# Deformable convolution of one Trainium2 core: samples on 32x32 tiles, pixels by lanes, y offsets by transfers

## The chip, the cores and the metric

The kernel runs on one core of a Trainium2 chip. The metric is the device time of one execution in microseconds (us), lower is better. The kernel before took 5572.15 us (median of 3 runs, 5569.34 to 5579.46).

TensorE (PE in the profile, with its weight loads in a row of their own, PEld) multiplies, VectorE (DVE), ScalarE (ACT) and GpSimd (POOL) work element by element, and SyncE (SP) issues nearly all transfers. Each engine runs its own instructions in order and waits for the others by semaphores.

## The reference, cut to what matters

```python
x = x + _L0_conv_ref(_gn(x), w_off, b_off, w_def)    # layer 0: the change is here
x = x + _L1_conv_ref(_gn(x), W)                      # scan over rows with a 9-tap convolution
x = x + _L2_conv_ref(_gn(x), ...)                    # messages
x = x + _L3_conv_ref(_gn(x), ...)                    # gated triangle product

def _L0_conv_ref(x, w_off, b_off, w_def):            # x: [4, 128, 128, 128]
    offset = einsum('bchw,oc->bohw', x, w_off) + b_off      # 72 = 4 groups x 9 taps x {dy, dx}
    py = offset[dy] + ky - 1 + row ; px = offset[dx] + kx - 1 + column
    val = bilinear sample of x[group] at (py, px)    # 32 channels per group, zero outside
    return relu(einsum('bgckhw,ogck->bohw', val, w)) # 3x3 convolution over the samples
```

`_gn` is a group norm with 32 groups. A bilinear sample is a sum over pixels of tent(y distance) x tent(x distance) x pixel, with tent(d) = max(0, 1 - |d|); the kernel uses this form.

## The kernel before

The four layers run one after the other. The deformable layer (`deform_layer`, line 181) takes the first 3300 us of the span or so. The two layers after it, and a general path for far offsets that lies in a branch not taken, are not touched.

*Blocks.* `deform_layer` walks over 172 blocks, 4 images x 43 blocks of 3 rows (RY = 3). Within a block the 130 padded columns fall into pieces of 4 (RX = 4), 33 of them. An output of a piece can only see 5 x 6 = 30 pixels (SY x SX, NS), called lanes, in each of 4 groups: 120 lanes. So the samples of a piece are one matmul (`sample`, line 521): 120 lanes x 128 channels of pixels as weights, whose blocks off the diagonal of groups are zero, and 120 x 108 products of tents `m` (9 taps x 3 rows x 4 columns) as the moving operand, in f32. One block has 33 of them, in 8 steps `i` of four (the last of five), each step into one PSUM tile `v_ps`, of which there are two. `keep_samples` (ACT, line 531) copies a step's tile to `v`.

*Tents.* The offsets, split into three bf16 parts each with the maximum of each beside it, lie in DRAM (`offs`). `load_places` brings them for a block, shifted by tap, into four groups of 25 partitions of `places` (2 tap slots x {y, x}). `spread_offsets` (line 498) turns them into tents on the 120 lanes by small bf16 matmuls with 25 rows: per tap three for y (130 columns) and four for x (99 columns with a stride of 4), 63 for a block, into tiles `t_ps` of two banks, two of them. The taps come in five batches (`SLOTS`: four of two taps, one of one), at steps given by `DONE`. `tents` then copies the y part out of PSUM (ACT, line 508) and multiplies it with the x part into `m` (DVE, line 510), once for each of the 9 taps.

*Convolution.* `convolved` is a generator: 15 f32 matmuls over `v` of the block before and the present one (line 579), cut into pieces of 3, 2, 2, 2, 2, 2, 2 and an end (line 552, DVE: relu and residual). Each step takes one piece.

*Preparing.* `prepared` runs beside it, one step at a time (`step`), at least 2 rows and mostly up to 26 rows ahead: it transposes 4 rows of x (line 370), norms them (ACT, line 373), writes 8 rows as table `tab` in DRAM with each pixel at its lanes (lines 378 and 380, pieces of 512 B, from `rows`), and computes the offsets: the product (line 385), corrections on DVE and POOL (390, 393), the bf16 parts (409, 415, 418), their range (412, 414), and after 8 rows a transfer to `offs`. `load_pixels` (line 466) gathers a block's pixel tile from `tab` in pieces of 128 B (33 x 120), into one of two tiles.

*Order.* The order of instructions on every engine is the order in which the Python code issues them (`manual_schedule`, line 680). For each block n the loop issues: the pixel load of block n+1; then for i in 0..7: at i = 3 `load_row(n + 2)` (the `places`), the spread batch due for block n+1, `keep_samples` of the step before, one piece of the convolution, `sample`, the multiplies of the batch, group norm statistics (`count`), and one or two steps of `prepared`. The engines' own queues are in this order too; SP issues the loads and the stores in it.

Of the kernel before, what the change touches and what calls it, by code (L numbers as in the profile page):

```python
# [42 lines left out]
LANES = NS * NG  # L43
# [6 lines left out]
SLOTS = [(0, 6), (1, 7), (2, 8), (3, 5), (4,)]  # L50
# [130 lines left out]
def deform_layer(tc, c, small, x, w_off, b_off, w_def, x1, tabs, offs):  # L181
# [13 lines left out]
    NB = RY * PADW  # L195
    with ExitStack() as ctx:
        wp = ctx.enter_context(tc.tile_pool(name="l0w", bufs=1))
        ps_g = ctx.enter_context(tc.tile_pool(name="l0ps_g", bufs=1, space=PSUM))
        ps_t = ctx.enter_context(tc.tile_pool(name="l0ps_t", bufs=2, space=PSUM))
# [4 lines left out]
        NPH = NPY + NPX  # L204
        keep = ctx.enter_context(tc.tile_pool(name="l0keep", bufs=2))
# [9 lines left out]
        places = [wp.tile([P, len(SLOTS), RY, OW], BF16, name=f"places_{i}") for i in range(3)]  # L215
        last = wp.tile([P, 3, 1, OW], BF16, name="places_last")
        pixels = [wp.tile([P, NXB + 1, P], F32, name=f"pixels_{i}") for i in range(2)]
        parts = wp.tile([2 * NL, NPART, 2 * RO * OW], BF16, name="parts")

        def rims():  # L220

            zero = two.tile([P, 2 * SX * P], F32, name="zero", tag="m")
            nc.vector.memset(zero, 0.0)
            zrow = zero[0 : NXB + 1]
            zoff = zero[0 : 2 * NL, 0 : NPART * OW].bitcast(BF16)
            zoff = zoff.rearrange("p (n l) -> p n l", n=NPART)
            for b in range(B):
                t = tabs[b].rearrange("x (r s) c -> x r s c", s=SX)
                nc.scalar.dma_start(
                    t[:, 0:2].rearrange("x r s c -> x (r s c)"), zrow  # L230
                )
                nc.scalar.dma_start(
                    t[:, S + 2 : S + 3].rearrange("x r s c -> x (r s c)"), zrow[:, 0 : SX * P]
                )
                for xb, s0, s1 in ((0, 0, 2), (NXB, 2, SX)):
                    nc.scalar.dma_start(
                        t[xb : xb + 1, 2 : 2 + S, s0:s1].rearrange("x r s c -> (x r) (s c)"),
                        zero[0:S, 0 : (s1 - s0) * P],
                    )
                rows_ = offs[b].rearrange("(p n) l -> p n l", n=NPART)  # L240
                nc.scalar.dma_start(rows_[:, :, 0 : 2 * OW], zoff)
                nc.scalar.dma_start(rows_[:, :, (S + 2) * OW :], zoff)

        def tables():

            awayi = two.tile([NG, NPH, LANES], I32, name="awayi", tag="x1c")
            for i in range(NPY):
                nc.gpsimd.iota(
                    awayi[:, i], pattern=[[0, NG], [1, SY], [0, SX]], base=-1 - i,
                    channel_multiplier=0,  # L250
                )
            for i in range(NPX):
                nc.gpsimd.iota(
                    awayi[:, NPY + i], pattern=[[0, NG * SY], [1, SX]], base=-1 - i,
                    channel_multiplier=0,
                )
# [5 lines left out]
                fill=64.0, base=0, channel_multiplier=-NS,  # L262
# [3 lines left out]
                fill=64.0, base=NS - 1, channel_multiplier=NS,  # L266
            )
            picks = one.tile([NG, 3, 4, 32], F32, name="picks", tag="rows")
            for i, sign in enumerate((-1.0, 1.0, 1.0)):
                nc.gpsimd.memset(picks[:, i], sign)  # L270
# [17 lines left out]
            for t in (*pixels, parts):  # L288
                nc.gpsimd.memset(t, 0.0)
            yield  # L290
            picks16 = one.tile([NG, 3, P], BF16, name="picks16", tag="ve")
            nc.vector.tensor_copy(picks16, picks.rearrange("g k q r -> g k (q r)"))
            kinds = two.tile([NG, 3, NPH * LANES], BF16, name="kinds", tag="m")
# [10 lines left out]
            n = NPH * LANES // 3  # L304
            for h in range(3):
                if h % 2 == 0:
                    tp = ps_t.tile([P, 2, 512], F32, name="t_ps")
                at = slice(h * n, (h + 1) * n)
                for i in range(3):
                    nc.tensor.matmul(  # L310
                        tp[:, h % 2, 0:n], lhsT=picks16[:, i], rhs=kinds[:, i, at],
                        start=i == 0, stop=i == 2,
                    )
                nc.scalar.copy(to[:, at], tp[:, h % 2, 0:n])
# [43 lines left out]
        def prepared(b, y0):  # L358

            table = tabs[b].rearrange("x (r s) c -> x r s c", s=SX)  # L360
# [4 lines left out]
            for h in range(0, RC, RO):  # L365
                if h % (2 * RO) == 0:
                    rows = one.tile([P, 2 * RO, P], F32, name="rows")
# [5 lines left out]
                nc.scalar.activation(rows[:, h0 : h0 + RO], pt, AF.Identity, bias=t, scale=s)  # L373
                if h0:
                    r0 = 2 + y0 + h - RO
                    for q in range(RX):
                        src = rows[q:S:RX]
                        nc.sync.dma_start(table[0:NXB, r0 : r0 + 2 * RO, q + 2, :], src)
                        if q >= 2:
                            nc.sync.dma_start(  # L380
                                table[1 : NXB + 1, r0 : r0 + 2 * RO, q - 2, :], src
                            )
# [6 lines left out]
                off = one.tile([2 * NL, RO, S], F32, name="off")  # L389
# [8 lines left out]
                p0 = h % (2 * RO)  # L398
                at = slice(p0 * OW, (p0 + RO) * OW)

                def to(i):
                    return parts[:, i, at].rearrange("p (r c) -> p r c", c=OW)[:, :, 2 : S + 2]

                def high(t):
                    halves = t.rearrange("p r c -> p (r c)").bitcast(BF16)
                    return halves.rearrange("p (r c two) -> p r c two", r=RO, two=2)[:, :, :, 1]

                rest = one.tile([2 * NL, RO, S], F32, name="rest")
                nc.scalar.copy(to(0), high(off))
                nc.gpsimd.tensor_tensor(rest, off, high(off), ALU.subtract)  # L410
                flat = off.rearrange("p r c -> p (r c)")
                nc.vector.tensor_reduce(ranges[:, 0, n : n + 1], flat, AX.X, ALU.max)
                yield
                nc.vector.tensor_reduce(ranges[:, 1, n : n + 1], flat, AX.X, ALU.min)
                nc.scalar.copy(to(1), high(rest))
                nc.gpsimd.tensor_tensor(to(2), rest, high(rest), ALU.subtract)
                yield
                nc.vector.tensor_scalar(
                    parts[:, NSPLIT:, at], parts[:, 0:NSPLIT, at], 0.0, None, ALU.max
                )  # L420
                if p0:
                    r0 = y0 + h - p0 + 2
                    nc.sync.dma_start(
                        offs[b].rearrange("(p n) l -> p n l", n=NPART)[
                            :, :, r0 * OW : (r0 + 2 * RO) * OW
                        ],
                        parts,
                    )
                    ready[b] = y0 + h + RO
                    yield  # L430
                yield

        def shifted(b, d, k, n, row, count):

            ky, kx = divmod(k, 3)
            wide = (S + 4) * OW
            first = (d * NK + k) * NG * NPART
            whole = offs[b]
            return bass.AP(
                whole.tensor, whole.offset + first * wide + (row - ky + 2) * OW + 2 - kx,  # L440
                [[wide, NG * NPART], [NG * NPART * wide - 1, n], [1, count]],
            )

        def load_places(b, j):
            t = places[(b * NYB + j) % 3]
            for d in range(2):
                for q, slot, k, n in ((0, 0, 0, 3), (0, 3, 3, 2), (1, 0, 6, 3), (1, 3, 5, 1)):
                    p1 = 64 * d + 32 * q + 1
                    nc.sync.dma_start(
                        t[p1 : p1 + KROWS - 1, slot : slot + n].rearrange("p k r c -> p k (r c)"),  # L450
                        shifted(b, d, k, n, RY * j, RY * OW),
                    )
            if j + 1 == NYB:
                for d in range(2):
                    p1 = 64 * d + 33
                    nc.sync.dma_start(
                        last[p1 : p1 + KROWS - 1].rearrange("p k r c -> p k (r c)"),
                        shifted(b, d, 6, 3, PADW - 1, OW),
# [3 lines left out]
        def load_pixels(b, j):  # L462
            t = pixels[(b * NYB + j) % 2]
            for g in range(NG):
                nc.sync.dma_start(
                    t[g * NS : (g + 1) * NS, :, g * CG : (g + 1) * CG],
                    tabs[b][:, RY * SX * j : RY * SX * j + NS, g * CG : (g + 1) * CG].rearrange(
                        "x l c -> l x c"
                    ),
                )  # L470
# [3 lines left out]
        def spread_offsets(src, slot, taps, rows):  # L474

            tps, todo = [], []
            for q in taps:
                tp = ps_t.tile([P, 2, 512], F32, name="t_ps")
                tps.append(tp)
                for d in range(2):  # L480
                    p0 = 64 * d + 32 * q
                    wide = OW if d else PADW
                    to = tp[0:LANES, d, 0 : rows * wide].rearrange("p (r c) -> p r c", c=wide)
                    mov = src[p0 : p0 + KROWS, slot]
                    if d == 0:
# [1404 lines left out]
```

## Time and profile before

| | |
|---|---|
| median of 3 runs | 5572.15 us |
| profiled execution: its own time, its span | 5567.76 us, 5565.9 us |
| mean granted TensorE clock | 0.971 |
| deformable layer, in the span | up to about 3300 us |
| busy: PE, PEld | 93%, 80% |
| busy: DVE, ACT, POOL | 55%, 49%, 14% |
| 700 to 2900 us (120 blocks, counted by their outputs): one block | 18.33 us |

The profile is one execution, recorded by the hardware. A row such as "L521 PE MATMUL v_ps<-m,pixels 120\*128 120x108 f32 x11352 | 1462.3, 273 | 3.6" names the line of the kernel, the engine, the operation, output and inputs, the shapes, how many, then busy time in us and the mean of one in ns, and the idle time just before with what ended it. An f32 matmul leaves two pairs of records (a weight load and a matmul each), a bf16 matmul one. Matmuls overlap, so that a mean of 273 ns is how long one is in the pipeline, and not how far apart two of them start; for that, the start times of single records are compared.

### The profile page before, as it was taken

The page shows a single profiled execution, that of the slowest core. Times are in us where ns is not written, and L with a number is a line of the kernel's source. Part 1 is how long each engine was busy: PE and PEld are TensorE (multiplying, and loading weights), DVE is VectorE, ACT ScalarE, POOL GpSimd, SP SyncE. Part 2 cuts the span into 40 slices and gives each one's busy share as a digit, 9 for nine tenths or more (in the row PEclk, how much of TensorE's full clock was granted, in tenths as well). Part 3 has the DMA queues.
Part 4 walks back from the last instruction along what each step waited for, and adds up shares of the span by engine and source line. Part 5 has one row for each costly group of instructions (what it writes and reads, how often), then busy time and mean ns, then how long its engine had stood idle before and what let it go on. Part 6 is the DMA issues. An engine that isn't in the chain of part 4 may idle for free. (4 is left out here: it accounts for less than half of the span.)

```text
span 5565.9 us, 112097 instructions
## 1 busy us (share of the span) xinstructions
PE 5163.0 (93%) x42401; PEld 4438.1 (80%) x42401; DVE 3079.9 (55%) x10450; ACT 2721.1 (49%) x5802; POOL 787.0 (14%) x698
## 2 busy tenths in 40 slices
PE   2899999999999999999999989999989889898896
PEld 1778888888888888888888878999967768577686
DVE  6544444554444644444433337888876574764844
ACT  1345555445554455554544432333345475664755
POOL 2021111001111011111100002222210010110102
PEclk9899999999999999999999989999989999999999
DMA  4555555555555555554543423233232352642525
GB/s 142 146 129 137 128 136 122 127 118 135 133 131 119 131 112 137 129 141 113 124 78 76 76 56 91 91 107 103 91 100 92 97 195 80 207 147 82 203 95 169
DMA packets 1138394, 671.46 MB, mean 121 GB/s; under 512 B 737133, under 2 KB 1003566, under 8 KB 1121206
## 3 DMA queue, kind: packets, MB, share of 16 engines
q1 hardware_dynamic: 1127664, 657.77, 45.2%
q8 instruction: 338, 5.54, 0.4%
q10 hardware_dynamic: 10182, 6.43, 0.4%
q14 instruction: 210, 1.72, 0.1%
HBM read 382.88 MB, written 281.11 MB: 119 GB/s over the span
## 5 line engine op out<-in xcount | busy, mean ns | idle before, releaser
L510 DVE TENSOR_TENSOR m<-ty,t_ps 120x390 f32<-120x390 f32 x1548 | 805.0, 557 | 1497.2 <-ACT ty L508 1496.0
L521 PEld LDWEIGHTS v_ps<-m,pixels 120*128 120x128 f32 x11352 | 1436.1, 194 | 86.0 <-issue 8.7
L521 PE MATMUL v_ps<-m,pixels 120*128 120x108 f32 (+1 forms) x11352 | 1462.3, 273 | 3.6 <-ACT v L531 3.5
L531 ACT COPY v<-v_ps 128x432 f32<-128x432 f32 x1376 | 719.7, 523 | 1268.7 <-PE v_ps L521 1265.8
L579 PE MATMUL conv_ps<-v,wdef 128*128 128x128 f32 (+2 forms) x5160 | 1301.8, 378 | 6.5 <-DVE x1c L552 5.9
L579 PEld LDWEIGHTS conv_ps<-v,wdef 128*128 128x128 f32 x5160 | 812.8, 192 | 256.0 <-issue 21.7
L508 ACT COPY ty<-t_ps 120x390 f32<-120x390 f32 x1560 | 688.2, 489 | 176.9 <-PE t_ps L498 169.5
L498 PE MATMUL t_ps<-places,spread 25*120 25x99 bf16 (+1 forms) x10836 | 520.0, 259 | 62.1 <-DVE m L510 37.8
L498 PEld LDWEIGHTS <-spread 25*120 25x120 bf16 x10896 | 338.9, 136 | 224.5 <-issue 124.6
L1639 PEld LDWEIGHTS proj_ps<-wcat,X 128*128 128x128 f32 x4096 | 473.2, 192 | 19.1 <-issue 18.9
L393 POOL TENSOR_TENSOR off<-off,koff 72x512 f32<-72x512 f32 x128 | 162.1, 1266 | 2294.1 <-DVE off L390 2215.8
L1639 PE MATMUL proj_ps<-wcat,X 128*128 128x128 f32 x4096 | 481.3, 276 | 0.0
L1072 ACT ACTIVATE rowT<-x1T_ps,t_x,s_x 128x128 f32<-128x128 f32 x512 | 192.7, 457 | 366.4 <-PE x1T_ps L1065 342.8
L1085 PE MATMUL m_ps<-carry,w 128*128 128x172 f32 x2286 | 361.5, 311 | 0.0
L1646 DVE TENSOR_TENSOR L<-proj_ps,work 128x256 f32<-128x256 f32 x256 | 108.6, 424 | 430.0 <-ACT work L1643 429.9
L1085 PEld LDWEIGHTS m_ps<-carry,w 128*128 128x128 f32 x2286 | 345.5, 188 | 0.0
L1185 POOL TENSOR_TENSOR sum_h<-sum_h,x2c 128x512 f32<-128x512 f32 x128 | 163.2, 1275 | 1159.4 <-DVE x2c L1145 1159.4
L1736 POOL TENSOR_TENSOR gate<-normed,gate 128x512 f32<-128x512 f32 x128 | 163.4, 1276 | 1127.8 <-ACT normed L1735 867.2
L1643 ACT ACTIVATE work<-proj_ps 128x512 f32<-128x512 f32 x256 | 152.1, 598 | 293.2 <-PE proj_ps L1639 287.8
L1746 PE MATMUL out_ps<-outw,gate 128*128 128x128 f32 x1024 | 190.2, 288 | 30.3 <-POOL gate L1736 30.3
L1746 PEld LDWEIGHTS out_ps<-outw,gate 128*128 128x128 f32 x1024 | 162.9, 200 | 38.9 <-POOL gate L1736 38.9
L1449 PE MATMUL self_ps<-R,ws 128*128 128x512 f32 x256 | 147.3, 680 | 32.4 <-DVE X L1460 17.3
(237 smaller groups left out, 6499.6 us busy)
## 6 DMA issues: line engine op xcount, KB each, us to landing
pixels<-tab SPq DMA_DIRECT2D x688, 123.8 KB
xin<-in_x_dram SPq DMA_DIRECT2D x56, 1024.0 KB
off<-parts SPq DMA_DIRECT2D x64, 891.0 KB
tab<-rows SPq DMA_DIRECT2D x384, 128.0 KB
places<-off SPq DMA_DIRECT2D x688, 55.7 KB
x<-x1c SPq DMA_DIRECT2D x32, 1024.0 KB
x1rows<-x SPq DMA_DIRECT2D x128, 256.0 KB
x2T<-x2c SPq DMA_DIRECT2D x128, 256.0 KB
```

The costliest lines, as they stand in the source:

```text
L498: nc.tensor.matmul(to, lhsT=spread[p0 : p0 + KROWS, ph, :], rhs=mov, start=True, stop=True,)
L508: nc.scalar.copy(ty[:, 0:n], tp[0:LANES, 0, 0:n])
L510: nc.vector.tensor_tensor(m, ty[:, 0:n].rearrange("p (r c) -> p r c", c=PADW), tx, ALU.mult)
L521: nc.tensor.matmul(vp[:, h * n : h * n + rows * w].rearrange("p (k c) -> p k c", c=w), lhsT=pix[0:LANES, xb, :], rhs=m[:, :, RX * xb : RX ...
L531: nc.scalar.copy(v[:, :, c0 : c0 + 4 * RX].rearrange("p k (h c) -> p k h c", c=RX), vp[:, 0 : 4 * n].rearrange("p (h k c) -> p k h c", h=4 ...
L579: nc.tensor.matmul(pc[:, at : at + r1 - r0, :], lhsT=wdef[:, 3 * ky + kx, :], rhs=v[:, k0 + kx, r0:r1, kx : kx + S], start=m == 0, stop=m ...
L1072: nc.scalar.activation(rt[:, b, :], px[:, b, :], AF.Identity, bias=t, scale=s)
L1085: nc.tensor.matmul(to, lhsT=wgt, rhs=src[:, :, at : at + n], start=i == 0, stop=i + 1 == len(todo),)
L1185: nc.gpsimd.tensor_tensor(sum_h, sum_h, x2c[:, :, i], add)
L1639: nc.tensor.matmul(pp[:, j], lhsT=X[:, j0 + j, :], rhs=wcat[:, cols], start=True, stop=True)
L1736: nc.gpsimd.tensor_tensor(gt, a, gt, ALU.mult)
L1746: nc.tensor.matmul(po[:, j], lhsT=a[:, j], rhs=outw, start=False, stop=True)
```

## The change

All of it is in `deform_layer` and its tables in DRAM.

1. *Samples.* The lanes of a group are padded from 30 to 32 (`LG`), so that group g stands on partitions 32g to 32g+29 both in `pixels` and in the tents. A sample of a piece becomes four f32 matmuls, one for each group, with 30 rows, 32 output channels and 108 columns, on the four diagonal 32x32 tiles of TensorE. All four write the same PSUM tile, each to its own 32 partitions. The pixel tile has [128, 33, 32] instead of [128, 33, 128] elements; there are three of them, and no zero blocks.
2. *Pixels by lanes.* The table in DRAM is laid out as [chunk of 8 rows, group, row, lane column, piece, channel], so that one lane's pixels of all 33 pieces are one run of 4224 B. `load_pixels` reads 120 such runs by 4 or 8 transfers. Writing the table takes six transfers per 8 rows, as before, in pieces of 128 B.
3. *y offsets of the first two rows of taps by transfers.* `offys` in DRAM keeps these y offsets in f32, three times, shifted by the column tap. `load_places` brings each row of them to the 32 lanes of its group (4 transfers of 64 pieces of 4752 B). ACT adds the lane's own y and takes the absolute value in place (`across`, three per block), DVE subtracts one and cuts at zero (`lowered`, one per block), which gives minus the tent. Only the third row of taps still gets its y tents from TensorE.
4. *Spread in three batches.* A batch has one column tap: twelve x matmuls (three row taps on three groups of partitions, 99 columns) and three y matmuls on the fourth group (132 columns), 45 for a block, into one `t_ps` of four banks, of which there is one. `tents` copies one y part and multiplies 2 x 396 elements by one DVE instruction and 396 by another.
5. *Convolution in longer runs.* Two pieces at each even step, none at odd steps.
6. *Order.* `load_row(n + 2)` at i = 1 instead of 3; spread batches for block n+1 at i = 2, 4, 6; `across` at i = 0 (one) and 1 (two), `lowered` at i = 1. `offs` (x parts and the third row's y parts alone) and `offys` are written every 4 rows.
7. *Start.* The rims of the new tables are zeroed by more ACT transfers.

```diff
-LANES = NS * NG
+LG = 32
+LANES = LG * NG
-        ps_t = ctx.enter_context(tc.tile_pool(name="l0ps_t", bufs=2, space=PSUM))
+        ps_t = ctx.enter_context(tc.tile_pool(name="l0ps_t", bufs=1, space=PSUM))
-        places = [wp.tile([P, len(SLOTS), RY, OW], BF16, name=f"places_{i}") for i in range(3)]
+        places = [wp.tile([P, KS, RY, OW], BF16, name=f"places_{i}") for i in range(2)]
+        tent = [wp.tile([LANES, KS, RY, KS, OW], F32, name=f"tent_{i}") for i in range(4)]
-        pixels = [wp.tile([P, NXB + 1, P], F32, name=f"pixels_{i}") for i in range(2)]
+        pixels = [wp.tile([P, NXB + 1, CG], F32, name=f"pixels_{i}") for i in range(3)]
...
+                for kx in range(KS):
+                    nc.sync.dma_start(
+                        offys[b][:, r0 : r0 + RO, kx, :],
+                        wide[2 * NG * kx : 2 * NG * (kx + 1), :, 2 - kx : 2 - kx + OW],
+                    )
...
         def load_places(b, j):
...
+            for q, (first, ky) in enumerate(from_):
+                nc.sync.dma_start(
+                    y[q * LG : (q + 1) * LG, 0 : KS - 1].rearrange("p i r k c -> p i (r k c)"),
+                    same_on_lanes(b, q, RY * j),
+                )
+                nc.sync.dma_start(
+                    t[32 * q + 1 : 32 * q + KROWS].rearrange("p k r c -> p k (r c)"),
+                    shifted(b, first, ky, RY * j, RY * OW),
+                )
...
-        def spread_offsets(src, slot, taps, rows):
+        def spread_offsets(src, rows, taps):
+            tp = ps_t.tile([P, KS + 1, 512], F32, name="t_ps")
+            ph0 = 0 if rows == RY else RY
+            for i in range(NPX):
+                cs = slice(i, OW, RX)
+                for q in (*taps, KS):
+                    at = slice(32 * q, 32 * q + KROWS)
+                    to = tp[0:LANES, q, 0 : rows * OW].rearrange("p (r c) -> p r c", c=OW)
+                    if q < KS:
                         nc.tensor.matmul(
+                            to[:, :, cs], lhsT=spread[at, NPY + i, :], rhs=src[at, :, cs],
                             start=True, stop=True,
                         )
+                    elif i < rows:
+                        nc.tensor.matmul(
+                            to[:, i], lhsT=spread[at, ph0 + i, :], rhs=src[at, i],
+                            start=True, stop=True,
+                        )
+        def across(n, r):
+            t = tent[n % 4][:, 0 : KS - 1, r].rearrange("p k x c -> p k (x c)")
+            nc.scalar.activation(t, t, AF.Abs, bias=lane_y[:, r : r + 1])
+        def lowered(n):
+            t = tent[n % 4][:, 0 : KS - 1]
+            nc.vector.tensor_scalar(t, t, 1.0, 0.0, ALU.subtract, ALU.min)
...
-                nc.tensor.matmul(
-                    vp[:, h * n : h * n + rows * w].rearrange("p (k c) -> p k c", c=w),
-                    lhsT=pix[0:LANES, xb, :], rhs=m[:, :, RX * xb : RX * xb + w],
-                    start=True, stop=True,
-                )
+                for g in range(NG):
+                    at = slice(g * LG, g * LG + NS)
+                    nc.tensor.matmul(
+                        vp[g * CG : (g + 1) * CG, h * n : h * n + rows * w].rearrange(
+                            "p (k c) -> p k c", c=w
+                        ),
+                        lhsT=pix[at, xb, :], rhs=m[at, :, RX * xb : RX * xb + w],
+                        start=True, stop=True,
+                    )
...
-                if i == 3:
+                if i == 1:
                     load_row(n + 2)
-                todo = advance(NB_ * (n + 1) + DONE[i])
+                kx = i // 2 - 1
+                batch = more and i in (2, 4, 6)
+                if batch:
+                    tp = spread_row(n + 1, kx)
                 if vps is not None:
                     keep_samples(*vps)
-                next(convs, None)
+                if i % 2 == 0:
+                    next(convs, None)
+                    next(convs, None)
                 vps = sample(m, pix, i, NK * RY), vk, i, NK * RY
-                multiply(todo)
+                if more and i < 2:
+                    for r in range(i, 2 * i + 1):
+                        across(n + 1, r)
+                if more and i == 1:
+                    lowered(n + 1)
+                if batch:
+                    multiply(n + 1, kx, tp)
```

## The prediction

> **What bounds the kernel now.** I read the shares of busy time and the slices first, then the windows, the groups, the waits and the timeline, and last the start times of single records.
>
> ```profile
> PE 5163.0 (93%) x42401; PEld 4438.1 (80%) x42401; DVE 3079.9 (55%) x10450; ACT 2721.1 (49%) x5802; POOL 787.0 (14%) x698
> ...
> PE   2899999999999999999999989999989889898896
> ...
> PEclk9899999999999999999999989999989999999999
> ```
>
> PE is busy at 90% or more in nearly every slice, at an almost full granted clock, so the clock gives nothing back. The windows over 120 blocks of the deformable layer say it more sharply (columns: us; busy PE, PEld, DVE, ACT, POOL; clock; DMA share, GB/s):
>
> ```profile
> 1250.00:1800.00 550.00, 545.77 (x4937) 456.42 (x4938) 254.24 (x627) 290.67 (x629) 100.22 (x90) 0.98 0.57 131
> 1800.00:2350.00 550.00, 544.20 (x5011) 458.14 (x5011) 281.26 (x886) 285.89 (x620) 73.51 (x66) 0.99 0.56 127
> ```
>
> PE 99%, DVE about 50%, ACT 52%, DMA 57%: only PE sets the pace. What it does, by groups:
>
> ```profile
> L521 PEld LDWEIGHTS v_ps<-m,pixels 120*128 120x128 f32 x11352 | 1436.1, 194 | 86.0 <-issue 8.7
> L521 PE MATMUL v_ps<-m,pixels 120*128 120x108 f32 (+1 forms) x11352 | 1462.3, 273 | 3.6 <-ACT v L531 3.5
> ...
> L579 PE MATMUL conv_ps<-v,wdef 128*128 128x128 f32 (+2 forms) x5160 | 1301.8, 378 | 6.5 <-DVE x1c L552 5.9
> ...
> L498 PE MATMUL t_ps<-places,spread 25*120 25x99 bf16 (+1 forms) x10836 | 520.0, 259 | 62.1 <-DVE m L510 37.8
> ```
>
> The sample is the largest. Idle before these rows is small, so a shorter wait is worth little; fewer or cheaper matmuls are worth their time. The timeline shows how they alternate, and one of the rare stalls:
>
> ```profile
> 1502.64 1.04 PE L521 MATMUL v_ps<-m,pixels 120*128 120x108 f32 x8
> 1503.62 0.56 PE L498 MATMUL t_ps<-places,spread 25*120 25x130 bf16 x14
> 1504.11 0.71 PE L579 MATMUL conv_ps<-v,wdef 128*128 128x128 f32 x4
> 1504.65 1.04 PE L521 MATMUL v_ps<-m,pixels 120*128 120x108 f32 x8
> 1506.43 0.29 PE L498 MATMUL t_ps<-places,spread 25*120 25x130 bf16 x2 [0.73 <-DVE m L510]
> ```
>
> Start to start in the single records: two sample matmuls 111 ns (a load of 128 columns fills 107 of it, the 108 columns some 90); conv records 111, 216 and 323 ns for 128, 256 and 384 columns. A spread batch of 14 spans 0.29 us; its first four, on four row groups, start within 10 ns. The step from sample to spread takes 0.204 us, from spread to conv 0.196, each some 0.1 over the normal, and the first weights after it show another 0.107. A block of 18.33 us (2200 us / 120) is thus: sample 66 x 0.111 = 7.3, conv 30 records about 6.0, spread with its ten changes 3.2, transposes and offset products 1.0; rest 0.8 stalls and small steps.
>
> **The change, part by part, per block.**
>
> *Sample.* Out go 66 record pairs at 0.111, in come 264 in 66 groups of four. If four tiles run side by side as the four row groups of the spread do, a group takes its 108 columns, 90 ns ((323 - 216)/128 = 0.84 each), plus some 3, and the 32-column load (107 x 32/128 = 27 ns) hides: 66 x 0.093 = 6.1, so -1.2 us. No row shows a 32x32 tile; ends: the four in a row, 264 x 0.093 = 24.6 (+17 us), and nothing hidden better than the columns, 6.1. The nearest row is the spread's, with tiles of 32 rows, and I take 6.1.
>
> Here the Trainium skill speaks against. TensorE: Matmul & The Clock Gate, "Packing small matmuls", says that a weight load overlaps a running matmul only where the row group differs; a tile's next load has the same row group, so a group would take 27 + 90 = 117 ns, 66 x 0.117 = 7.7, a loss of 0.4 instead. The trace has loads of the same rows hidden: 107 + 90 would be 197 ns, the pairs stand 111 apart. The row decides.
>
> *Feeding PE.* PE instructions per block go from about 331 to about 700 (528 + 90 + 60 and the rest). 16.3 to 18 us for 700 is 23 to 26 ns each; no stretch of 256 in this trace runs under 49. The records bound the supply: after the wait at 217.394 us, 24 instructions up to the next wait at 217.562 were issued in 117 ns (5 ns each) with PE busy and ten still queued; after one at 4197.806, with PE idle, eight took 206 ns (26 each):
>
> ```profile
> 4197.88 0.42 PEld L1571 LDWEIGHTS turn_ps<-ident,X 128*128 128x128 f32 x4 [1.45 <-ACT X L1608]
> ```
>
> In the block PE is busy, so I take the first. By the same page's "Back-to-back issue gap", no two matmuls start under 25 ns apart: 264 x 25 = 6.6 for the sample, -0.7 instead of -1.2. Four spread starts within 10 ns go under it, so it isn't applied to tiles.
>
> *Spread.* 63 matmuls in 4.5 batches x 0.29 = 1.3 become three batches of four waves at 0.091 (the stride-4 wave's distance): 1.1, so -0.2. The one `t_ps` is written again two steps (some 4 us) later; ACT's 396-element copy (0.49) and DVE's multiplies lie within that, so the stall on DVE m (37.8 us / 172 = 0.2) goes: -0.2.
>
> *Changes of tiling.* Ten before. After: two at i = 0, three each at i = 2, 4, 6, and two around each transpose or offset product that stands between samples (1.5 per block): 14. Four more at 0.1 and half a weight load: +0.45. The longer conv runs are what keeps this from being more; they save nothing alone.
>
> *ACT.* Six copies fewer (6 x 0.49), three `across` of 792 more, at 0.84 (from 390 elements 0.491, 512 0.598): -0.4. The tightest place: at i = 1, two of them stand before the next `keep_samples`; 0.52 + 1.7 + 0.52 = 2.7 us, and PE needs that buffer only at i = 3, some 3.5 us on. Hidden; without cover 0.5 per block. *DVE.* Nine multiplies of 0.557 become three of 792 and three of 396 (0.97 and 0.56 at some 1 ns per element): 4.6 against 5.0; `lowered`, 2376 elements, 1.3 to 2.5 us: near 11 of 17 us busy. It is issued at i = 1, with `multiply` a step behind: hidden. *SP and DMA.* 15.6 transfers a block become about 20, at 0.4 to 0.65 us of SP: 10 to 13 us, still under the block. `load_row` goes ahead of two steps' preparation stores, waits for offsets written many rows ago, and leaves `across` 7/8 of a block, 15 us, for the landing. 3960 pieces of 128 B go, some 1700 of 128 B and 256 of 4752 B (1.2 MB) come: the share stays near 0.5 to 0.6. Nothing on the path.
>
> *Start.* Some 50 more ACT transfers at 0.8 to 1.0 us. Before, they ended at 35 us and ACT's next work waited for later inputs up to 77: 0 to +30 us, I take +10.
>
> Sum: -1.2 - 0.2 - 0.2 + 0.45 = -1.15 us; x 172 = -198; + 10 = -188. From the profiled execution's 5567.8 (span 5565.9 and 2 around it) that leaves 5380; the median of the runs lies 4 above that execution: **5385 us**. Own range 5280 to 5500: the floor of 25 ns gives back 86, a load chain of four 27-ns loads (107 ns a group) 160, and stalls and small steps of 0.8 a block (138 us in all) could shrink by up to 100 more.
>
> **Rivals.** (A) *Instruction supply becomes the bound*, slower. It decides from 700 x t > 18.3 + 1.15, about 25 ns an instruction sustained. At 26 (the idle-PE figure) the block needs at least 18.2 us. The queue holds some 32, so a sample step with no conv before it takes 64 x 0.026 = 1.7 us instead of 0.74, and one behind a conv about 1.0: 4 x 1.7 + 4 x 1.0 = 10.8 for the sample instead of 6.1, 21.9 a block. At 31 (load to matmul in that stretch) the block needs 21.7 to 24. With 18.5 to 23: 5600 to 6380, say 6000. For: nothing here sustains under 49. Against: the 5 ns. Chance 0.24. (B) *The four tiles don't run side by side*, as all write one PSUM bank, which the spread's four do not: +17 a block, 8500 us. But each writes its own 32 partitions of it, so 0.07. (C) *The tile's load is exposed*, +0.4 + 0.05 a block: about 5650; 0.07. (D) *The gain is eaten by ACT, DVE or a late transfer* and nothing changes, 5560 to 5580: 0.03; against it the shares of one half. (Likeliest: 0.59.)
>
> **How the numbers follow.** Faster: 0.59. Same (within 0.2%, what a measurement here can tell from no change): 0.03. Slower: A, B, C, 0.38. The range leaves out B, the upper tenth of A and a little below: 5290 to 6250.
>
> **What would show it.** Right: sample groups of four start within some 10 ns and 93 ns apart, PE stays at 99% of the window, blocks of 17.2 us. A: gaps put down to issue before the sample's loads, matmul starts 50 ns or more apart. B: tile starts 90 ns apart. C: groups 117 apart. Wrong otherwise if PE idles before the sample for ACT v or DVE, or before the block for `tent` or pixels.

## The result, and the profile after

The changed kernel takes 5738.21 us (median of 4 runs, 5731.17 to 5750.83) against 5574.16 us before on the same chip: 1.0297 times as long (95% interval 1.0275 to 1.0318). Forecast were 5385 us and a gain. The profiled execution took 5742.03 us, its span is 5740.3 us, 174 us longer than before.

From the page of the changed kernel, the parts that were read of before:

```profile
PE 4957.1 (86%) x74156; PEld 3969.5 (69%) x74156; DVE 3226.0 (56%) x10107; ACT 2713.1 (47%) x5285; POOL 765.9 (13%) x702
...
PE   1688899888898898888888997999998989899896
...
PEclk9889999999999999999999998999999999999999
```

PE is busy for 206 us less, though it executes 74156 pairs instead of 42401. It now has holes: 8 in the slices where 9 stood. The windows over the same stretch:

```profile
1250.00:1800.00 550.00, 493.26 (x9862) 360.42 (x9851) 267.51 (x547) 273.81 (x510) 87.75 (x81) 0.95 0.75 171
1800.00:2350.00 550.00, 481.33 (x10163) 363.90 (x10161) 292.92 (x811) 265.50 (x502) 58.46 (x54) 0.94 0.75 175
```

PE is busy for 88 to 90% of them instead of 99, the granted clock is 0.94 to 0.95 instead of 0.98 to 0.99, the DMA share 0.75 instead of 0.57. DVE is busy for 12 to 13 us more in each window, ACT for 17 to 20 us less, so both are still half idle. The groups (L557 and L553 are new, the y tents):

```profile
L580 PE MATMUL v_ps<-tent,pixels 30*32 30x108 f32 (+1 forms) x45408 | 1250.3, 255 | 86.9 <-ACT v L592 40.2
L640 PE MATMUL conv_ps<-v,wdef 128*128 128x128 f32 (+2 forms) x5160 | 1277.3, 392 | 14.5 <-DVE x1c L613 11.7
...
L557 DVE TENSOR_SCALAR tent<-tent 128x2376 f32<-128x2376 f32 x172 | 242.2, 1408 | 694.5 <-ACT tent L553 596.7
L566 DVE TENSOR_TENSOR tent<-tent,t_ps 128x792 f32<-128x792 f32 x516 | 502.0, 973 | 196.9 <-ACT ty L563 187.8
L553 ACT ACTIVATE tent<-tent,lane_y 128x792 f32<-128x792 f32 x516 | 474.8, 954 | 105.6 <-DMA tent<-offy 52.8
...
L540 PE MATMUL t_ps<-places,spread 25*128 25x99 bf16 x6192 | 289.0, 276 | 231.0 <-DVE tent L567 212.2
```

The number to look at is idle before: at the spread (L498 before, L540 now) it rose from 62 to 231 us, nearly all of it put down to DVE's multiplies (L567), and at the sample from 4 to 87 us.

Two kinds of holes (stretches in which PE stands idle) lie behind it. One comes in nearly every block. PE's timeline of one (other spreads, convolution and transposes are left out):

```profile
1508.37 0.94 PE L580 MATMUL v_ps<-tent,pixels 30*32 30x108 f32 x32
1509.88 0.94 PE L580 MATMUL v_ps<-tent,pixels 30*32 30x108 f32 x32 [0.57 <-ACT v L597]
...
1513.76 0.94 PE L580 MATMUL v_ps<-tent,pixels 30*32 30x108 f32 x32 [0.52 <-ACT v L592]
...
1516.63 0.26 PE L540 MATMUL t_ps<-places,spread 25*128 25x99 bf16 x3 [1.34 <-DVE tent L567]
```

and ACT and DVE in the same stretch:

```profile
1508.69 0.62 ACT L447 COPY parts<-offwide 72x512 bf16<-72x512 bf16 x1 [2.44 <-POOL offwide L432]
...
1511.50 1.80 ACT L553 ACTIVATE tent<-tent,lane_y 128x792 f32<-128x792 f32 x2
1513.20 0.51 ACT L592 COPY v<-v_ps 128x432 f32<-128x432 f32 x1
1513.60 0.49 ACT L563 COPY ty<-t_ps 128x396 f32<-128x396 f32 x1
```

```profile
1513.33 1.40 DVE L557 TENSOR_SCALAR tent<-tent 128x2376 f32<-128x2376 f32 x1 [3.37 <-ACT tent L553]
1514.65 0.56 DVE L461 TENSOR_SCALAR parts<-parts 72x1584 bf16<-72x1584 bf16 x1
1515.13 0.97 DVE L566 TENSOR_TENSOR tent<-tent,t_ps 128x792 f32<-128x792 f32 x1
1516.02 0.56 DVE L567 TENSOR_TENSOR tent<-ty,t_ps 128x396 f32<-128x396 f32 x1
```

The copy of the sample's PSUM tile (L592) stands behind two `across` (L553); `lowered` (L557) waits for the last of them, the multiplies (L566, L567) wait for `lowered`, and the spread at i = 4 needs the one `t_ps` that they read.

The other kind is rarer and longer. PE, SP and ACT, from one timeline:

```profile
1546.91 0.94 PE L580 MATMUL v_ps<-tent,pixels 30*32 30x108 f32 x32
...
1547.39 0.60 SPq L464 DMA_DIRECT2D off<-parts  x1
...
1551.58 0.62 ACT L447 COPY parts<-offwide 72x512 bf16<-72x512 bf16 x1 [6.78 <-DMA off<-parts]
...
1552.11 0.51 ACT L592 COPY v<-v_ps 128x432 f32<-128x432 f32 x1
...
1552.77 1.66 PE L580 MATMUL v_ps<-tent,pixels 30*32 30x108 f32 x32 [4.92 <-ACT v L597]
```

The transfer `off<-parts` (issue to landing some 4 us) holds ACT at a copy of the preparation, the sample's copies are queued behind it, and PE stands for 4.9 us. The transfer was issued late, too. SP had stood in front of it for 6.6 us until a load of `places` landed, which had been issued at 1540.24, behind the four y transfers of that block. SP's waits of this kind between 700 and 2900 us (in total, times, longest):

```profile
SPq L464 <- DMA places<-off: 105.6, 35, 7.0
```

In the kernel before they are 24.6 us, and in c2 below, without the y transfers, 33.0. In other blocks it is the load of `xin` that PE waits for (9 times, up to 8 us between 700 and 2900 us).

### The profile page after: what moved, and what is told of

The parts are those of the page before. It is cut to its first block, busy times and chain, and to the rows that moved or that the text cites. A ratio compares the mean times of both kernels' runs of the same rounds, so it can differ in the third digit from the quotient of the medians.

```text
span 5740.3 us, 177391 instructions
## 1 busy us (share of the span) xinstructions
PE 4957.1 (86%) x74156; PEld 3969.5 (69%) x74156; DVE 3226.0 (56%) x10107; ACT 2713.1 (47%) x5285; POOL 765.9 (13%) x702
## 5 line engine op out<-in xcount | busy, mean ns | idle before, releaser
L580 PE MATMUL v_ps<-tent,pixels 30*32 30x108 f32 (+1 forms) x45408 | 1250.3, 255 | 86.9 <-ACT v L592 40.2
L640 PE MATMUL conv_ps<-v,wdef 128*128 128x128 f32 (+2 forms) x5160 | 1277.3, 392 | 14.5 <-DVE x1c L613 11.7
L580 PEld LDWEIGHTS v_ps<-tent,pixels 30*32 30x32 f32 x45408 | 1046.1, 106 | 334.6 <-issue 118.4
L592 ACT COPY v<-v_ps 128x432 f32<-128x432 f32 x1376 | 714.2, 521 | 1084.2 <-PE v_ps L580 1072.4
L557 DVE TENSOR_SCALAR tent<-tent 128x2376 f32<-128x2376 f32 x172 | 242.2, 1408 | 694.5 <-ACT tent L553 596.7
L566 DVE TENSOR_TENSOR tent<-tent,t_ps 128x792 f32<-128x792 f32 x516 | 502.0, 973 | 196.9 <-ACT ty L563 187.8
L553 ACT ACTIVATE tent<-tent,lane_y 128x792 f32<-128x792 f32 x516 | 474.8, 954 | 105.6 <-DMA tent<-offy 52.8
L432 POOL TENSOR_TENSOR offwide<-offwide,koff 72x512 f32<-72x512 f32 x128 | 150.6, 1176 | 2593.4 <-DVE offwide L429 1930.8
L540 PE MATMUL t_ps<-places,spread 25*128 25x99 bf16 x6192 | 289.0, 276 | 231.0 <-DVE tent L567 212.2
L540 PEld LDWEIGHTS <-spread 25*128 25x128 bf16 x6240 | 158.1, 108 | 367.6 <-DVE tent L567 257.0
L613 DVE SCALAR_TENSOR_TENSOR x1c<-conv_ps,xres 128x384 f32<-128x384 f32 (+2 forms) x192 | 96.8, 511 | 533.1 <-PE conv_ps L640 513.4
L563 ACT COPY ty<-t_ps 128x396 f32<-128x396 f32 (+1 forms) x528 | 255.8, 484 | 292.2 <-PE t_ps L540 238.0
```

Of the source, the lines that this page charges most:

```text
L540: nc.tensor.matmul(to[:, :, cs], lhsT=spread[at, NPY + i, :], rhs=src[at, :, cs], start=True, stop=True,)
L553: nc.scalar.activation(t, t, AF.Abs, bias=lane_y[:, r : r + 1])
L557: nc.vector.tensor_scalar(t, t, 1.0, 0.0, ALU.subtract, ALU.min)
L563: nc.scalar.copy(ty[:, 0:n], tp[0:LANES, KS, 0:n])
L566: nc.vector.tensor_tensor(loaded, loaded, tx[:, 0 : KS - 1], ALU.mult)
L580: nc.tensor.matmul(vp[g * CG : (g + 1) * CG, h * n : h * n + rows * w].rearrange("p (k c) -> p k c", c=w), lhsT=pix[at, xb, :], rhs=m[at, ...
```

## The experiments

The table counts every kernel alike, from its records between 700 and 2900 us: blocks by the copies of `v`, PE's idle time as gaps between its matmuls, and the time at half the clock from the granted clock. All but the median and the share are us per block. c1, c2, c3 and d3 leave out part of the y tents, so that they show what a part costs and do not compute the layer.

| kernel | median, us | block | PE busy | PE idle | at half clock | DMA share |
|---|---|---|---|---|---|---|
| before | 5574 | 18.37 | 18.16 | 0.21 | 0.46 | 0.55 |
| after | 5738 | 19.22 | 17.03 | 2.19 | 2.06 | 0.76 |
| a1_tents_early | 6004 | 20.86 | 17.48 | 3.39 | 3.72 | 0.71 |
| a2_two_parts | 5748 | 19.24 | 17.03 | 2.22 | 2.03 | 0.76 |
| a3_short_conv | 5709 | 18.98 | 17.42 | 1.57 | 1.30 | 0.77 |
| b1_tiles_only | 5588 | 18.52 | 18.23 | 0.29 | 0.32 | 0.54 |
| b2_tiles_long_conv | 5542 | 18.25 | 17.62 | 0.63 | 0.48 | 0.54 |
| c1_no_tent_work | 5591 | 18.33 | 16.76 | 1.57 | 1.61 | 0.80 |
| c2_no_y_transfers | 5563 | 18.27 | 16.69 | 1.58 | 1.19 | 0.46 |
| c3_neither | 5268 | 16.30 | 15.96 | 0.33 | 0.28 | 0.49 |
| d1_early_and_far | 5592 | 18.35 | 16.79 | 1.57 | 1.57 | 0.76 |
| d2_far_and_xin2 | 5510 | 17.93 | 16.59 | 1.35 | 1.06 | 0.79 |
| d3_early_no_transfers | 5329 | 16.62 | 16.07 | 0.55 | 0.39 | 0.49 |
| d4_extra_step | 5505 | 17.77 | 16.50 | 1.27 | 1.10 | 0.78 |

**First: order, buffers, or the tiles?** Theory 1 was that PE's idle comes from where the new ACT and DVE work stands; theory 2, that the new transfers make data late.

a1 moves the y tents up by a third of a block.

```diff
-                if more and i < 2:
-                    for r in range(i, 2 * i + 1):
-                        across(n + 1, r)
-                if more and i == 1:
-                    lowered(n + 1)
+                if n + 2 < len(blocks) and i >= 5:
+                    across(n + 2, i - 5)
+                    if i == 7:
+                        lowered(n + 2)
```

> The changed kernel with one edit: the y tents (three across on ACT, one lowered on DVE) are made for block n+2 at steps 5, 6, 7 of block n, instead of for block n+1 at its steps 0 and 1. Theory 1 (order on ACT and DVE): the spread at i = 4 waits 1.35 us a block because lowered, and behind it the two multiplies, come late behind across; that wait goes, PE idle falls from 2.2 to about 1.0 us a block, and the time by 1.1 to 1.4 us x 172 blocks to 5500-5550 us. Theory 2 (transfers: the DMA share rose from 0.55 to 0.75 and data come late): no change, 5720-5750 us.

Measured: 6003.95 us, 1.0759 times before (1.0739 to 1.078). Neither theory had this. What ACT waited for in that kernel (us in total, times, longest):

```profile
ACT v L592 <- PE v_ps L580: 680.8, 428, 6.9
ACT tent L553 <- DMA tent<-offy: 234.8, 47, 11.4
```

In the changed kernel the second row has 40.5 us and 10 times. The y transfers, issued at step 1, have often not landed at step 5; ACT then waits in front of the sample's copies. So the work can't be moved alone: the transfers give it its place. The wait that a1 was to remove did go (PE's gaps from a sample to a spread fell from 120 us to 14), but a larger one came: 247 us of PE's waits before samples for ACT's copy of `v`, instead of 14.

a2 doubles the tiles at which ACT and POOL stood in the long hole.

```diff
+                wide, parts = wide2[h // RO % 2], parts2[h // RO % 2]
                 off = wide[:, :, 2 : S + 2]
```

> The changed kernel with one edit: parts and offwide, the tiles that the preparation fills every 4 rows and that wait for their own transfers to DRAM before they are written again, are doubled. Theory 1: the stalls of PE of over 2 us (27 in 115 blocks, 93 us, 0.8 us a block) come from ACT and POOL standing at these tiles with keep_samples queued behind them; most of them go, 5600-5650 us. Theory 2: the late transfers are the load of the share itself, and the same stalls appear elsewhere: 5720-5750 us.

Measured: 5747.95 us, 1.0313 (1.0296 to 1.033), as the changed kernel. There are no fewer long holes (30 over 2 us, 107 us in all, instead of 27 and 93), and PE waits 44 us for `xin` instead of 38: the single tile was where the lateness showed, not its source.

b1 and b2 take the tiles to the kernel before.

```diff
-                    lhsT=pix[0:LANES, xb, :], rhs=m[:, :, RX * xb : RX * xb + w],
+                        lhsT=pix[at, xb, :], rhs=m[at, :, RX * xb : RX * xb + w],
...
-                next(convs, None)
+                if i % 2 == 0:
+                    next(convs, None)
+                    next(convs, None)
```

> The kernel before with lanes padded to 32, pixels without zero blocks, samples on four diagonal 32x32 tiles, and the convolution taken by two pieces at even steps; tents, batches and transfers as before. If the tiles are worth what the sample's records show (66 groups of 93 ns for 66 pairs of 111: -1.2 us a block) and only changes of tiling cost (16 against 10, one half us): 5440-5480 us. If the uneven steps are what starves PE (ACT copies of a step come together): 5570 us and more.

> As b2_tiles_long_conv, with the convolution by one piece at each step as before. By the count of changes of tiling (24 against 10, at 0.1 us, and four more first weights at 0.107): +1.8 - 1.2 = +0.6 us a block, 5650-5700 us. If changes of tiling cost little, as b2: below 5500 us.

(The last four lines of the diff belong to b2 alone.) Measured: b2 5542.11 us, 0.994 (0.9924 to 0.9957); b1 5588.21, 1.0029 (1.0019 to 1.0039). Both times lie between the two that were expected. The tiles work: the four of a group start within 19 ns, the next group 95 ns after, and the sample's spacings (from one matmul's start to the next) fall from 6.75 to 6.1 us a block. Changes of tiling cost less than was counted (b1 is 0.15 us a block longer, not 0.6), and in b2, with uneven steps, PE idles 0.4 us more than before. So the tiles with the longer runs are worth some 30 us by themselves, the tiles alone cost 15; neither explains a loss of 164.

**Second: the two halves of the y chain.** c1 leaves out `across` and `lowered`, c2 the transfers, c3 both.

```diff
-                        across(n + 1, r)
...
-                    lowered(n + 1)
```

```diff
-                nc.sync.dma_start(
-                    y[q * LG : (q + 1) * LG, 0 : KS - 1].rearrange("p i r k c -> p i (r k c)"),
-                    same_on_lanes(b, q, RY * j),
-                )
```

> The changed kernel without across (ACT) and lowered (DVE) in the blocks; the y offsets are still transferred, and the y tents of two rows of taps are left out of what is computed. Theory 1 (the 2.9 us of ACT and 1.4 us of DVE a block stand ahead of the copies and multiplies that PE waits for): the waits at the spread and at the samples go, PE idle falls from 2.2 to below 0.8 us a block, the granted clock rises to 0.97, 5400-5470 us. Theory 2 (the y transfers, share 0.75, make the other loads late): the stalls of more than 2 us stay, 5620-5740 us.

> The changed kernel without the transfers that bring the y offsets of two rows of taps to the lanes (the tents start from zeros and what is computed from them is left out in that sense); across and lowered run as before on what stands there. Theory 2: DMA share back to about 0.5, late loads and stores gone, 5560-5620 us. Theory 1: only the long stalls shrink, the waits of 1.35 and 0.5 us a block stay, 5650-5720 us.

> The changed kernel without both: neither the y transfers nor across and lowered (the y tents of two rows of taps are left out of what is computed). PE's own work is unchanged. If it is right that this work is 1.2 us a block less than before and all the loss lies in the y chain: 5370-5420 us. If the uneven steps (two conv pieces at even steps, none at odd ones) or the tiles starve PE by themselves: above 5500 us.

Measured: c1 5590.87 us (1.004, 1.0027 to 1.0053), c2 5563.13 us (0.9993, 0.9985 to 1.0001), c3 5268.0 us (0.946, 0.9441 to 0.9478). Either half alone costs about 2.0 us a block over c3 (18.3 against 16.3), both 2.9. c3 lies 102 us below its range: PE's own work fell by more than the 1.2 us that were counted. The waits differ in kind. PE of c1, with the transfers and without the tent work:

```profile
PE img_ps L403 <- DMA xin<-in_x_dram: 49.4, 11, 9.8
...
PE t_ps L540 <- DVE tent L567: 24.7, 18, 4.5
```

PE of c2, with the tent work and without the transfers:

```profile
PE t_ps L536 <- DVE tent L563: 143.1, 108, 3.5
...
PE img_ps L403 <- DMA xin<-in_x_dram: 1.8, 1, 1.8
```

Besides these, ACT of c1 waits 73 us at its copy L447 for `off<-parts` (16 times, up to 8.9 us), with the sample's copies behind it. Each theory is right for one half. Theory 1 claimed too much: c1 was to take 5470 us at most. c2 lies in the range that theory 2 gave it, but the waits at the spread, which theory 1 named, stayed. c3's windows show what PE does when nothing is late:

```profile
1250.00:1800.00 550.00, 534.34 (x11709) 407.15 (x11707) 290.25 (x861) 230.38 (x482) 74.83 (x69) 0.98 0.51 131
1800.00:2350.00 550.00, 539.78 (x11552) 404.15 (x11546) 262.18 (x589) 241.48 (x499) 100.83 (x93) 0.99 0.52 125
```

11.6 to 11.7 thousand pairs in 550 us instead of 9.9 to 10.2: without the y chain, the uneven steps, the single `t_ps` and the instruction stream leave PE idle for only 0.33 us a block.

a3 takes the convolution back to a piece at each step.

```diff
-                if i % 2 == 0:
-                    next(convs, None)
-                    next(convs, None)
+                next(convs, None)
```

> The changed kernel with the convolution by one piece at each step again. If uneven steps are what lets PE catch up with ACT and DVE: idle falls below 1 us a block, but 8 more changes of tiling and four more first weights cost 1.2 us: 5730-5780 us. If the y chain is late by itself, the idle stays and the changes add: 5850-5950 us. If changes of tiling are cheap, below 5700 us.

Measured: 5709.05 us, 1.0243 (1.0221 to 1.0264): 29 us faster than the changed kernel. It falls between the times expected: PE idles 0.6 us a block less, but not below 1, and is busy 0.39 longer, less than the 1.2 counted for changes (the clock, which is higher, hides part of them). So the longer runs, a gain in b2 over b1, are a loss here. That even steps give the late y chain more cover would explain it, but no run shows that.

**Third: can both be mended?** Theory 3: the tent work is hidden when it is early, but only if its transfers are earlier still.

d1 is a1 with the y transfers one block sooner, and with all four of them behind the loads of `places` instead of between them. d2 is d1 with two `xin` tiles and asks for the next one four rows sooner. d3 is a1 without the y transfers. d4 is d2 with one more step before ACT's first copy. (The tent work moves as in a1; of the other edits these are the main lines.)

```diff
                     load_row(n + 2)
+                    load_y(n + 3)
...
```

```diff
-            xc = one.tile([P, RC, S], F32, name="xin")
+            xc = two.tile([P, RC, S], F32, name="xin")
...
-                if h + RO == RC:
+                if h + 2 * RO == RC:
                     look_ahead(b)
```

> As a1_tents_early, but the y transfers go out one block sooner (for block n+3 at step 1 of block n), so that they have 1.5 blocks, not half a block, to land before across. Theory 3 (both at once: ACT and DVE stand ahead of PE's copies, and moving them up only meets transfers that have not landed): the 1.35 us at the spread goes and ACT no longer waits for the y offsets; what stays are the late xin loads and longer queues of the share 0.75, about 0.5 us a block: 5480-5560 us. If the transfers slow ACT, DVE or PE otherwise than by being late: 5650 us and more.

> As d1_early_and_far, with two xin tiles (the 1 MB load of the next 16 rows is asked for four rows sooner), since PE waits 0.33 us a block for it in the changed kernel and 0.41 in c1_no_tent_work. Theory 3: another 0.3 to 0.6 us a block with the clock that comes back, 5380-5470 us, near what was forecast. If not a late load but the order of SP's queue is behind it: as d1.

> The changed kernel without the y transfers (as c2_no_y_transfers, the y offsets of two rows of taps are left out) and with the tents made early as in a1. Theory 3: ACT's 2.9 and DVE's 1.4 us a block are hidden when they do not stand between a spread and the next, so the time is near that of c3_neither, 5270-5310 us. If the work itself is too much for ACT or DVE: near c2, 5500 us and more.

Measured: d1 5592.35 us (1.004, 1.0029 to 1.0051), 146 us faster than the changed kernel and as fast as c1, which has no tent work at all: done early, the tent work adds nothing that can be seen beside its transfers. Without the transfers it still costs 61 us: d3 takes 5329.37 us (0.9568, 0.9552 to 0.9584), 19 above its range, and 16.62 us a block against the 16.30 of c3. d2, 5509.68 us (0.9889, 0.9853 to 0.9925), beats the kernel before. d1 missed its range by 32 us, d2 by 40: the transfers cost 1.7 us a block (d1 over d3), not the 0.5 that was allowed for them. In d1 SP's waits for `places` at L464 fell to 0.5 us, from 92 in a1 and 141 in c1. So two things changed between a1 and d1, the lead of the y transfers and their place in SP's queue, and no run has one without the other. The DMA share in d2:

```profile
1250.00:1800.00 550.00, 515.25 (x10878) 385.83 (x10870) 288.00 (x572) 295.79 (x563) 98.66 (x88) 0.97 0.80 188
```

```diff
                 yield
+                yield
                 n = (b * S + y0 + h) // RO
```

> As d2_far_and_xin2, with one more step of the preparation between the offset's last add on POOL and ACT's first copy of it, so that ACT does not stand at that copy (96 us of ACT's waits in 120 blocks) with keep_samples behind it. If that wait is what is left of PE's idle (1.4 us a block, most of it before samples for ACT v): 5440-5490 us. If what is left are late transfers: as d2, 5495-5525 us.

Measured: 5504.86 us (0.9889, 0.9872 to 0.9905), as d2, though ACT's wait at that copy for POOL fell from 96 to 39 us. What is left between d2 or d4 (17.8 to 17.9 us a block) and d3 (16.6) goes with the transfers, and this wait is not most of it. Through what it goes, the 1.2 MB of y offsets a block on the DMA engines or the order in which SP issues all transfers, was not told apart; a smaller y transfer was not tried.

## Why the prediction was wrong, by its own steps

**Sample, right.** The groups of four stand 92.5 ns apart in the changed kernel, the four starts of one within 20 ns. Loads of the same tile hide: rivals B and C, and the Trainium skill's rule behind C (TensorE: Matmul & The Clock Gate, "Packing small matmuls"), are not what these records show. One sample step of 32 pairs in the changed kernel (in c3 such a step takes 0.94 us, too):

```profile
1512.30 0.94 PE L580 MATMUL v_ps<-tent,pixels 30*32 30x108 f32 x32
```

These are eight groups. The last matmul is 0.25 of the 0.94 us in the pipeline; the starts before it fill the rest, 0.117 for the first group after a change of tiling and 0.0925 for each further one.

**Feeding PE, right.** Rival A, the likeliest of the slower ones, did not come: the 64 instructions of such a step start within 0.69 us, 11 ns apart, and c3 as a whole runs 700 in 16.3 us. Two figures of this rival were off without deciding anything. The densest 256 instructions of the kernel before are 44 ns apart, not 49. And the 25 ns above which supply becomes the bound belong to 18.3 - 1.15, not to 18.3 + 1.15.

**Spread and changes of tiling, too small a gain.** The sum of PE's own work was -0.95 a block (-1.2 - 0.2 + 0.45). Busy time fell by 2.2 from before to c3. The spread, counted from start to start with the steps into and out of it, took 4.05 us before, not 3.2, and 2.17 in c3. A batch cost less than was counted (0.28 us of spacings, not 0.36), and with three batches instead of five, two of these steps in and two out went whole. The steps between sample and convolution became fewer (8.5 a block with 1.5 us before, where they needed no change of tiling; 4.7 with 1.1 us in c3). Together these outweigh the +0.45.

**ACT and DVE "hidden", wrong: this step failed.** It set the two `across` against the time until PE needs the buffer, by durations alone, with ACT free at the step's start. ACT was not free: in the block shown above it stood for 2.44 us, until 1508.69, at the copy L447, behind POOL. And "multiply a step behind: hidden" looked at DVE's load; what counts is the chain across - across - lowered - two multiplies, 1.8 + 1.4 + 0.6 (L461) + 1.5 us in a row, which ends at the only `t_ps`. Where the sum had -0.2 for a stall that goes, PE's idle time rose by 2.0, together with the next step's share; this step alone, without the transfers, makes it 1.58 (c2) instead of 0.33 (c3) and a block 2.0 us longer. Nor did the stall go in c3 (idle 0.21 before, 0.33 in c3).

**SP and DMA "nothing on the path", wrong: this step failed, too.** The share was said to stay near 0.5 to 0.6. It became 0.75. The term was mis-sized: by their records, the 256 packets of 4752 B take 343 ns each, 88 us of the 16 engines' time in a block, and the 120 pixel runs 29; the 3960 small pieces that went had taken 60 (15 ns each). And a share below one was taken for free. In c1, at 0.80, `xin`, `places` and `off` land late often enough to cost 2.0 us a block over c3; on top of the tent work (c2 to the changed kernel) the transfers cost 0.95.

**The clock, not in the sum.** "The clock gives nothing back" was right, but a loss was not thought of. Time at half the clock rose from 0.46 to 2.06 us a block, and PE was busy for 0.45 and 1.71 of it. If its work takes twice as long there, half of the difference, 0.6 us (an estimate from these figures), is what the lower clock cost, about three quarters of the 0.85 us by which a block got longer.

**Start, too small.** +10 was taken, +37 came: the first samples are copied at 158.1 us instead of 121.0. ACT issues the transfers of the rims until 62 us instead of 34. PE and DVE wait for ACT's work behind them, and `std_x` follows some 43 us later, as it did before (at 104.7 instead of 77.4): the wait for "later inputs up to 77" was itself behind these transfers. The rest goes with the first y transfers: without them (c2) the first copy is at 148.7.

Together, a block: 18.37 - 2.2 (PE's own work, c3) + 1.98 (idle) + 1.07 (PE busy longer than in c3, 0.7 of it by the clock, estimated as above) = 19.22. That is +0.85; x 172 + 37 = 183, and 175 were measured at the last sample (3467.4 against 3292.2). The gain in PE's own work was there, larger than forecast; the y chain, which stands for 18 small matmuls and six copies a block, took 470 us (5738 - 5268).

## What to carry to other kernels

Moving work from the engine that is the bound to engines and transfers that are half idle pays only where their queues let it: follow the moved chain through each in-order queue to the buffer that the bound engine needs next, starting from when the queue is really free, not from its share of busy time. Work that depends on a transfer can be moved up only together with the transfer: a1 moved the work alone and lost, d1 moved both and gained. Look also at what stands behind the new transfers in the issuing queue. On TensorE a stall costs more than its length where it lowers the clock.

## What the runs showed of the hardware

In each of these traces every change of the granted clock lies on a grid of 3.413 us, within 3 ns. In the changed kernel between 700 and 2900 us, 33 windows of that grid at full clock had PE busy for less than half, and 31 of them were followed by a window at half the clock; of 30 between 0.5 and 0.6, 13 were; of 25 between 0.6 and 0.7, 4; of 487 above 0.7, none (in the kernel before, 3 of 622). In 27 of these 48 windows no single hole took half of the window: shorter ones, alone or together, were enough.

Four diagonal tiles that write the four 32-partition parts of one PSUM bank start 7 ns apart in the changed kernel: sharing the bank cost nothing that these records show.
